# Streams of a recurrence started together, with part of the z terms brought into PSUM by a matrix product

## The chip, the cores and the metric

The program runs on one NeuronCore of a Trainium2 chip. The metric is the device time of one execution in microseconds; the profile is one execution of its own, and its span runs from the first to the last instruction.

## What is computed

The input is x, 32 images of 128 channels by 64 x 64 pixels. A first layer (group norm, a convolution with kernels mixed per image) and a windowed attention layer with layer norms come first. They fill most of the program and are not touched. What the change touches is the last part, cut here from the reference:

```python
Wx = jnp.einsum('bti,hi->bth', x, W)              # 32 images, T = 4096 steps, 128 channels
Wx = ((flat - mean) * rsqrt(var + eps) * gamma + beta).reshape(B, T, H)
def step(yt, wx_t):
    yt = sigmoid(wx_t + yt @ V.T)
    return (yt, yt)
_, ys = lax.scan(step, zeros, swapaxes(Wx, 0, 1))
t = t + ys                                        # added to the result of the layers before
```

Every image is a chain of 4096 steps, one 128 x 128 product and one sigmoid each.

## The kernel before

Before the recurrence the image part writes z (the W product, not yet normalised) to DRAM as z_d and the value to which y is added to the output. The batch norm is folded into a per-channel factor scl and a shift shf.

**by_runs** is the recurrence that runs with these inputs; the other branch, by_steps, is not taken. It cuts the 4096 steps of an image into NRUN = 128 runs of RUN = 32 steps and does all runs at once, each run started WARM = 20 steps early from zero so that it forgets its start. A *group* g is NI = 2 images, so one step handles 128 channels by 2 x 128 values. A group therefore takes 20 + 32 = 52 steps, and there are 16 groups: 832 steps.

A warm step is, after the first one: a TensorE product with fVT (L1914), a VectorE operation that adds scl times z (L1915), and a ScalarE sigmoid (L1916). A kept step is the same on all 256 columns (L1920, L1921, L1924), and a POOL copy (L1925) that puts y over the z it came from. The first warm step is only a sigmoid of z (L1911). y alternates between two tiles, yw[0] and yw[1].

NSTR = 4 *streams* take the groups j, j+4, j+8, j+12 in turn. The order on every queue is the order in which the program emits: a loop calls the streams one after another, one step each. Stream j joins lag = 13 rounds after stream j-1, so the streams stay a quarter of a group apart from beginning to end.

**Transfers.** Six groups have room at a time: five zr tiles and the tile frames. load(g) issues two 2 MB transfers on the SP queue, DRAM to SBUF (L1891). When a group is done, POOL issues two transfers of 2 MB that add the group to the output in DRAM (L1928), and then SP is given load(g + 6), which goes into the tile that these two are still reading. So the chain for every tile is: last copy of group g, its two accumulating transfers, load of group g + 6, first sigmoid of group g + 6 (L1911).

```python
    load(g + NSTR + 2)

live = [stream(j) for j in range(NSTR)]
step = 0
lag = (WARM + RUN) // NSTR
while live:
    for st in list(live[: 1 + step // lag] if step < lag * NSTR else live):
```

Of the kernel before, what the change touches and what calls it, by code (L numbers as in the profile page):

```python
# [8 lines left out]
F32 = mybir.dt.float32  # L9
AF = mybir.ActivationFunctionType  # L10
ALU = mybir.AluOpType
AX = mybir.AxisListType

P = 128
# [19 lines left out]
RUN = 32  # L34
WARM = 20
NRUN = T // RUN
NI = 2
NSTR = 4
# [19 lines left out]
class Clock:  # L58
# [7 lines left out]
    def __init__(self, nc):  # L66
        self.nc = nc
        self.free = {e: 0.0 for e in self.ENGINES.values()}
        self.seen = {}
        self.place = {}  # L70
        self.slots = {}
        self.mode = None
        self.ring = 0.0
        self.port = [[], []]
        self.half, self.edge, self.used = 0, self.WINDOW, 0.0
# [71 lines left out]
    def take(self, eng, pool):  # L147
        t = min(pool, key=lambda t: self.after(eng, t, True))
        pool.remove(t)
        return t  # L150
# [106 lines left out]
def hybrid_kernel(  # L257
# [24 lines left out]
    nc = tc.nc  # L282
# [4 lines left out]
    of = out.rearrange("b c h w -> c b (h w)")  # L287
# [15 lines left out]
    ident = const.tile([P, P], F32, name="ident")  # L303
# [36 lines left out]
    fVT = const.tile([P, P], F32, name="fVT")  # L340
# [12 lines left out]
    with tc.tile_pool(name="sb1", bufs=1) as sb1, tc.tile_pool(  # L353
        name="ps1", bufs=1, space=bass.MemoryType.PSUM
# [32 lines left out]
    with tc.tile_pool(name="sb2", bufs=1) as sb2, tc.tile_pool(  # L387
        name="ps2", bufs=1, space=bass.MemoryType.PSUM
# [1462 lines left out]
    scl = const.tile([P, 1], F32, name="scl")  # L1851
    shf = const.tile([P, 1], F32, name="shf")
# [18 lines left out]
    def by_runs():  # L1871

        with ExitStack() as pb:
            zp = pb.enter_context(tc.tile_pool(name="zp", bufs=NSTR + 1))
            hp = pb.enter_context(tc.tile_pool(name="hp", bufs=1))
            p_v = pb.enter_context(tc.tile_pool(name="p_v", bufs=2, space=bass.MemoryType.PSUM))
            pb.enter_context(tc.manual_schedule())

            NG = NB // NI
            zs = {}

            def load(g):
                if g < NG:
                    if g % (NSTR + 2):
                        zs[g] = zp.tile([P, NI, NRUN, RUN], F32, name="zr")
                    else:
                        zs[g] = framed.rearrange("p i (c r) -> p i c r", r=RUN)
                    for i in range(NI if g else 0):  # L1890
                        nc.sync.dma_start(  # L1891
                            zs[g][:, i].rearrange("p c r -> p (c r)"), z_d[g * NI + i]
                        )

            for g in range(NSTR + 2):
                load(g)

            def stream(j):
                yw = []
                for i in range(2):  # L1900
                    yw.append(hp.tile([P, NI, NRUN], F32, name=f"yw{j}_{i}"))
                    nc.vector.memset(yw[i], 0.0)
                for g in range(j, NG, NSTR):
                    zt = zs[g]
                    if g >= NSTR:
                        for i in range(2):
                            nc.vector.memset(yw[i][:, :, 0:1], 0.0)
                    for r in range(RUN - WARM, RUN):
                        y, z = yw[r % 2][:, :, 1:], zt[:, :, 0 : NRUN - 1, r]
                        if r == RUN - WARM:  # L1910
                            nc.scalar.activation(y, z, AF.Sigmoid, bias=shf, scale=scl)  # L1911
                        else:
                            ps = p_v.tile([P, NI, NRUN], F32, name=f"v{j}")[:, :, 1:]
                            nc.tensor.matmul(ps, fVT, yw[1 - r % 2][:, :, 1:], start=True, stop=True)  # L1914
                            nc.vector.scalar_tensor_tensor(ps, z, scl, ps, ALU.mult, ALU.add)  # L1915
                            nc.scalar.activation(y, ps, AF.Sigmoid, bias=shf)  # L1916
                        yield
                    for r in range(RUN):
                        ps = p_v.tile([P, NI, NRUN], F32, name=f"v{j}")
                        nc.tensor.matmul(ps, fVT, yw[1 - r % 2], start=True, stop=True)  # L1920
                        nc.vector.scalar_tensor_tensor(  # L1921
                            ps, zt[:, :, :, r], scl, ps, ALU.mult, ALU.add
                        )
                        nc.scalar.activation(yw[r % 2], ps, AF.Sigmoid, bias=shf)  # L1924
                        nc.gpsimd.tensor_copy(zt[:, :, :, r], yw[r % 2])  # L1925
                        yield
                    for i in range(NI):
                        nc.gpsimd.dma_start(  # L1928
                            of[:, g * NI + i],
                            zt[:, i].rearrange("p c r -> p (c r)"),  # L1930
                            accum_op=ALU.add,
                            max_dma_last_dim=8192,
                        )
                    load(g + NSTR + 2)

            live = [stream(j) for j in range(NSTR)]
            step = 0
            lag = (WARM + RUN) // NSTR
            while live:
                for st in list(live[: 1 + step // lag] if step < lag * NSTR else live):  # L1940
                    try:
                        next(st)
                    except StopIteration:
                        live.remove(st)
                step += 1

    def by_steps():

# [50 lines left out]
    with tc.If(contr > 0) as arm:  # L1999
        by_runs()  # L2000
# [56 lines left out]
```

## Time and profile before

| what | value |
|---|---|
| device time, three executions | 4645.82, 4645.3, 4629.83 us (median 4645.3) |
| the profiled execution | 4639.78 us |
| its span | 4637.9 us |
| first sigmoid of the recurrence | 4049.6 us after the span's start |
| last sigmoid ends, last accumulating transfer issued | 4611.0 us, 4612.7 us |
| PE, DVE, ACT, POOL busy over the whole span | 90%, 77%, 54%, 36% |

The whole-span shares are averages over the image part (87% of the span) and the recurrence (the last 588 us), so they say nothing on this change. In the recurrence the rows to read are those with lines L1902 to L1928. PE has two records for each product in this data type. "Idle before" counts the time in which the engine had nothing before that row's instructions, with the one that ended it.

### The profile page before, as it was taken

How to read it: one execution, taken by the hardware profiler on the slowest of the kernel's cores; microseconds unless marked ns; L12 is line 12 of the kernel's file. 1: busy time of each engine (PE TensorE's matmuls, PEld its weight loads, DVE VectorE, ACT ScalarE, POOL GpSimd, SP SyncE). 2: the span in 40 equal slices, each digit the busy share in tenths (PEclk: the TensorE clock that was granted, in tenths of full speed). 3: DMA queues.
4: the chain of work that ended last, by engine and by line, in shares of the span. 5: the costliest groups of instructions: out<-in, count | busy, mean ns of one | idle time of the engine just before them, and what ended most of it. 6: DMA issues, size and time to landing. Idle time of an engine off the chain costs nothing.

```text
span 4637.9 us, 102446 instructions
## 1 busy us (share of the span) xinstructions
PE 4195.7 (90%) x41527; PEld 2063.1 (44%) x41527; DVE 3576.6 (77%) x5472; ACT 2503.6 (54%) x4012; POOL 1649.0 (36%) x1656
## 2 busy tenths in 40 slices
PE   3999989999999999999999999999999997389995
PEld 1444444444444444444444444444444443145552
DVE  5877778888878877878887877878788854469994
ACT  0455555555555555545555455555555565258883
POOL 2433333333333333333333333333333321037674
PEclk9999999999999999999999999999999998679997
DMA  3434464554555555555555455555555453439997
GB/s 79 134 120 145 149 198 164 172 175 149 177 167 178 180 161 172 171 163 176 170 177 182 145 190 154 166 173 179 176 159 174 160 182 134 168 151 248 281 263 145
DMA packets 468568, 789.39 MB, mean 170 GB/s; under 512 B 339040, under 2 KB 349296, under 8 KB 435312
## 3 DMA queue, kind: packets, MB, share of 16 engines
q1 hardware_dynamic: 459376, 715.56, 47.3%
q0 software_dynamic: 8704, 67.11, 7.1%
q8 instruction: 332, 5.44, 0.5%
q14 instruction: 156, 1.28, 0.1%
HBM read 499.06 MB, written 276.76 MB: 167 GB/s over the span
## 4 chain that ended last, share of the span: by engine, by line
PE 26%; DVE 15%; DMA 7%; issue 3%; ACT 2%; SPq 2%; POOL 1%; DVEq 0%; ACTq 0%; POOLq 0%
PE nm L241 13%; PE sc L241 6%; PE av L241 4%; DVE v L1921 4%; DVE zt L241 3%; DVE v L1915 2%; SPq L241 2%; DMA place<-r_d 2%; PE v L1920 1%; DMA zr<-z_d 1%; DVE frames L241 1%; DMA place<-x_d 1%; DVE u L241 1%; ACT yw L1924 1%; DMA out_dram<-zr 1%
## 5 line engine op out<-in xcount | busy, mean ns | idle before, releaser
L241 ACT ACTIVATE ex<-sc 128x1152 f32<-128x1152 f32 x896 | 1013.6, 1131 | 879.9 <-PE sc L241 859.3
L241 POOL TENSOR_TENSOR qe<-qs,mqk 128x576 f32<-128x576 f32 x448 | 601.1, 1344 | 864.8 <-PE sc L241 856.3
L241 PE MATMUL nm<-u,w 128*128 128x512 f32 x1536 | 809.1, 631 | 18.9 <-POOL w L241 18.9
L241 PE MATMUL sc<-qe,ks 32*128 32x288 f32 x7168 | 698.0, 459 | 80.4 <-ACT ext L241 33.3
L241 PE MATMUL av<-ex,VE 128*32 128x144 f32 x14336 | 631.0, 294 | 29.7 <-DVE avs L241 29.1
L241 PEld LDWEIGHTS sc<-qe,ks 32*128 32x128 f32 x7168 | 284.9, 185 | 621.5 <-issue 168.0
L241 PEld LDWEIGHTS av<-ex,VE 128*32 128x32 f32 x14336 | 368.1, 110 | 369.1 <-issue 260.8
L241 POOL TENSOR_TENSOR u<-frames 128x528 f32<-128x528 f32 x256 | 374.4, 1475 | 154.8 <-PE nm L241 152.3
L241 PE MATMUL nm<-u,h 128*128 128x512 f32 x768 | 393.0, 620 | 0.0
L241 PEld LDWEIGHTS nm<-u,w 128*128 128x128 f32 x1536 | 253.2, 191 | 276.0 <-issue 245.1
L1920 PE MATMUL v<-yw,fVT 128*128 128x256 f32 x1024 | 327.6, 442 | 40.3 <-ACT yw L1924 39.1
L241 ACT ACTIVATE place<-zt 128x1024 f32<-128x1024 f32 x256 | 264.1, 1054 | 142.4 <-DVE zt L241 121.2
L241 DVE SCALAR_TENSOR_TENSOR u<-u,u 128x528 f32<-128x528 f32 x256 | 263.1, 1044 | 66.8 <-POOL u L241 65.2
L1925 POOL COPY zr<-yw 128x256 f32<-128x256 f32 x416 | 258.7, 689 | 123.4 <-ACT yw L1924 122.7
L1924 ACT ACTIVATE yw<-v,shf 128x256 f32<-128x256 f32 x512 | 242.3, 474 | 106.0 <-DVE v L1921 68.3
L241 PE MATMUL nm<-zt,fWc 128*128 128x512 f32 x512 | 286.5, 651 | 7.8 <-ACT zt L241 6.8
L1921 DVE SCALAR_TENSOR_TENSOR v<-zr,scl,v 128x256 f32<-128x256 f32 x416 | 257.3, 665 | 40.7 <-PE v L1920 40.0
L241 POOL TENSOR_TENSOR kt<-ks,mqk 128x384 f32<-128x384 f32 (+1 forms) x96 | 86.3, 899 | 492.5 <-ACT ks L241 439.4
L241 PE MATMUL nm<-place,avg 128*32 128x256 f32 x3072 | 246.8, 401 | 8.2 <-ACT place L241 7.9
L1914 PE MATMUL v<-yw,fVT 128*128 128x254 f32 x608 | 212.1, 449 | 46.1 <-ACT yw L1911 28.2
L241 DVE SCALAR_TENSOR_TENSOR zt<-sc,gbk,zt 128x576 f32<-128x576 f32 (+1 forms) x192 | 174.9, 911 | 98.0 <-PE sc L241 95.6
L1920 PEld LDWEIGHTS v<-yw,fVT 128*128 128x128 f32 x1024 | 159.8, 194 | 194.6 <-ACT yw L1924 188.3
(205 smaller groups left out, 6676.8 us busy)
## 6 DMA issues: line engine op xcount, KB each, us to landing
place<-r_d SPq DMA_DIRECT2D x384, 512.0 KB
place<-in_conv_k_dram SPq DMA_DIRECT2D x128, 576.0 KB
x_d<-frames SPq DMA_DIRECT2D x32, 2112.0 KB
place<-x_d SPq DMA_DIRECT2D x128, 528.0 KB
frames<-in_x_dram SPq DMA_DIRECT2D x128, 512.0 KB
out_dram<-zt SPq DMA_DIRECT2D x64, 1024.0 KB
z_d<-zt SPq DMA_DIRECT2D x64, 1024.0 KB
zr<-z_d SPq DMA_DIRECT2D x26, 2048.0 KB
```

Of the source, the lines that this page charges most:

```text
L241: got = f(*args, **kw)
L1914: nc.tensor.matmul(ps, fVT, yw[1 - r % 2][:, :, 1:], start=True, stop=True)
L1915: nc.vector.scalar_tensor_tensor(ps, z, scl, ps, ALU.mult, ALU.add)
L1920: nc.tensor.matmul(ps, fVT, yw[1 - r % 2], start=True, stop=True)
L1921: nc.vector.scalar_tensor_tensor(ps, zt[:, :, :, r], scl, ps, ALU.mult, ALU.add)
L1924: nc.scalar.activation(yw[r % 2], ps, AF.Sigmoid, bias=shf)
L1925: nc.gpsimd.tensor_copy(zt[:, :, :, r], yw[r % 2])
```

## The change

The generator function becomes a class Stream, and the order of emission is chosen by an account: four clocks (PE, DVE, ACT, POOL), fixed costs for one operation of each, and a latency. At each turn the operation that can start earliest by this account is emitted, a single engine operation instead of a whole step. Four things differ in what the engines get:

- stream j is entered into the account at 10 us times j, instead of 13 rounds apart;
- a step may have its z term brought in by a second product, of z with dg, a diagonal matrix that holds scl, into the same PSUM tile ahead of the fVT product; the VectorE operation of that step is then left out. Group 0 may do so in any step; the other groups only while such products are at most 0.15 of the steps emitted;
- the two memsets of column 0 between two groups of a stream are emitted right after the last step of the group before, not ahead of the first step of the next;
- dg is made once by VectorE.

Products with fVT, sigmoids, copies, tiles, the pool of five zr tiles, the two accumulating transfers of a group and load(g + NSTR + 2) after them stay as they are.

```diff
+            dg = hp.tile([P, P], F32, name="dg")
+            nc.vector.tensor_scalar_mul(dg, ident, scl)
+            PE, DVE, ACT, POOL, LAT = 0.43, 0.56, 0.46, 0.64, 0.2
+            free = {"PE": 0.0, "DVE": 0.0, "ACT": 0.0, "POOL": 0.0}
...
+                    self.j, self.g, self.k, self.phase = j, j, 0, "ACT"
+                    self.at = 10.0 * j
...
+                def inject(self):
+                    k = self.k if self.phase == "PE" else self.k + 1
+                    c, r, z = self.step(k)
+                    self.ahead = p_v.tile([P, NI, NRUN], F32, name=f"v{self.j}")
+                    nc.tensor.matmul(self.ahead[:, :, c], dg, z, start=True, stop=False)
+                    take("PE", self.read[k % 2] + LAT, PE)
...
+                    if self.phase == "PE":
+                        whole = self.ahead is not None
+                        self.ps = self.ahead if whole else p_v.tile([P, NI, NRUN], F32, name=f"v{self.j}")
+                        self.ahead = None
+                        nc.tensor.matmul(self.ps[:, :, c], fVT, self.yw[1 - r % 2][:, :, c], start=not whole, stop=True)
+                        self.at = take("PE", self.at, PE) + 0.38
+                        self.phase = "ACT" if whole else "DVE"
+                        return
+                    if self.phase == "DVE":
+                        v = self.ps[:, :, c]
+                        nc.vector.scalar_tensor_tensor(v, z, scl, v, ALU.mult, ALU.add)
...
+                    if self.k == WARM + RUN:
+                        g = self.g
+                        for i in range(NI):
+                            nc.gpsimd.dma_start(
...
+                        load(g + NSTR + 2)
+                        self.g, self.k, self.phase = g + NSTR, 0, "ACT"
+                        if self.g < NG:
+                            for i in range(2):
+                                nc.vector.memset(self.yw[i][:, :, 0:1], 0.0)
...
-            live = [stream(j) for j in range(NSTR)]
-            step = 0
-            lag = (WARM + RUN) // NSTR
-            while live:
-                for st in list(live[: 1 + step // lag] if step < lag * NSTR else live):
...
+                    k = st.k if st.phase == "PE" else st.k + 1
+                    if st.ahead is not None or k >= WARM + RUN or (st.g and spent > 0.15 * steps):
+                        continue
+                    at = max(free["PE"], st.read[k % 2] + LAT, st.at if st.k == 0 else 0.0)
+                    if st.phase != "PE" and at + PE > st.due():
+                        continue
+                    if any(o is not st and at + PE > o.due() + 0.2 for o in live):
+                        continue
```

More of the change, by code (lines that the diff above doesn't have):

```diff
@@ L1896, in by_runs @@
                 load(g)
[L1898 to L1911, printed above, removed]
-                        else:
[L1913 to L1934, printed above, removed]
@@ L1936, in by_runs @@
-            live = [stream(j) for j in range(NSTR)]
-            step = 0
-            lag = (WARM + RUN) // NSTR
-            while live:
-                for st in list(live[: 1 + step // lag] if step < lag * NSTR else live):
[L1941 to L1945, printed above, removed]
+            dg = hp.tile([P, P], F32, name="dg")
+            nc.vector.tensor_scalar_mul(dg, ident, scl)
@@ new lines, in by_runs, with take, __init__, step @@
+            PE, DVE, ACT, POOL, LAT = 0.43, 0.56, 0.46, 0.64, 0.2
+            free = {"PE": 0.0, "DVE": 0.0, "ACT": 0.0, "POOL": 0.0}
+            def take(eng, at, cost):
+                at = max(at, free[eng])
+                free[eng] = at + cost
+                return at + cost
+            class Stream:
+                def __init__(self, j):
+                    self.j, self.g, self.k, self.phase = j, j, 0, "ACT"
+                    self.at = 10.0 * j
+                    self.ahead = self.ps = None
+                    self.read, self.kept = [-9.0, -9.0], [-9.0, -9.0]
+                    self.yw = []
+                    for i in range(2):
+                        self.yw.append(hp.tile([P, NI, NRUN], F32, name=f"yw{j}_{i}"))
+                        nc.vector.memset(self.yw[i], 0.0)
+                def step(self, k):
+                    warm = k < WARM
+                    c = slice(1, NRUN) if warm else slice(0, NRUN)
+                    r = RUN - WARM + k if warm else k - WARM
+                    z = zs[self.g][:, :, 0 : NRUN - 1, r] if warm else zs[self.g][:, :, :, r]
+                    return c, r, z
+                def due(self):
+                    if self.phase == "PE":
+                        return self.at
+                    if self.phase == "DVE":
+                        return max(self.at, free["DVE"]) + DVE + ACT + 2 * LAT
+                    return max(self.at, free["ACT"]) + ACT + LAT
+                def inject(self):
[4 more added lines that the diff above has]
+                    take("PE", self.read[k % 2] + LAT, PE)
+                def go(self):
+                    k = self.k
+                    c, r, z = self.step(k)
+                    y = self.yw[r % 2]
+                    if self.phase == "PE":
+                        whole = self.ahead is not None
[5 more added lines that the diff above has]
+                        return
+                    if self.phase == "DVE":
+                        v = self.ps[:, :, c]
+                        nc.vector.scalar_tensor_tensor(v, z, scl, v, ALU.mult, ALU.add)
+                        self.at = take("DVE", self.at, DVE) + 0.25
+                        self.phase = "ACT"
+                        return
+                    if k:
+                        nc.scalar.activation(y[:, :, c], self.ps[:, :, c], AF.Sigmoid, bias=shf)
+                    else:
+                        nc.scalar.activation(y[:, :, c], z, AF.Sigmoid, bias=shf, scale=scl)
+                    end = take("ACT", max(self.at, self.kept[k % 2] + LAT), ACT)
+                    self.read[k % 2] = end
+                    if k >= WARM:
+                        nc.gpsimd.tensor_copy(z, y)
+                        self.kept[k % 2] = take("POOL", end + LAT, POOL)
+                    self.at, self.phase, self.k = end + LAT, "PE", k + 1
+                    if self.k == WARM + RUN:
+                        g = self.g
+                        for i in range(NI):
+                            nc.gpsimd.dma_start(
+                                of[:, g * NI + i],
+                                zs[g][:, i].rearrange("p c r -> p (c r)"),
+                                accum_op=ALU.add,
+                                max_dma_last_dim=8192,
+                            )
+                        load(g + NSTR + 2)
+                        self.g, self.k, self.phase = g + NSTR, 0, "ACT"
+                        if self.g < NG:
+                            for i in range(2):
+                                nc.vector.memset(self.yw[i][:, :, 0:1], 0.0)
+                        else:
+                            live.remove(self)
@@ new lines, in by_runs @@
+            live = [Stream(j) for j in range(min(NSTR, NG))]
+            steps = spent = 0
+            while live:
+                best = None
+                for st in list(live):
+                    at = max(st.at, free[st.phase])
+                    if best is None or (at, st.g) < best[0]:
+                        best = (at, st.g), st, False
+                    k = st.k if st.phase == "PE" else st.k + 1
[6 more added lines that the diff above has]
+                        continue
+                    if (at, st.g) < best[0]:
+                        best = (at, st.g), st, True
+                _, st, ahead = best
+                if ahead:
+                    spent += 1
+                    st.inject()
+                else:
+                    steps += st.phase == "ACT"
+                    st.go()
```

## The prediction

> **What bounds the kernel now.** The change touches nothing before 4046 us, so the whole-span shares are left aside. I read the recurrence in stages (the view of busy time by stretch), then the groups, the chain of waits, and the DMA behind it.
>
> ```profile
> core 0: us, PE busy (x) PEld busy (x) DVE busy (x) ACT busy (x) POOL busy (x), PEclk, DMA share, GB/s
> 4047.90:4082.00 34.10, 15.74 (x26) 6.51 (x26) 8.94 (x16) 7.80 (x15) 0.00 (x0) 0.50 0.99 418
> ...
> 4230.00:4260.00 30.00, 29.48 (x107) 15.80 (x106) 29.81 (x56) 25.39 (x55) 21.70 (x38) 1.00 0.99 252
> ...
> 4615.00:4634.00 19.00, 0.00 (x0) 0.00 (x0) 0.00 (x0) 0.00 (x0) 0.00 (x0) 0.50 1.01 209
> ```
>
> With one stream the engines are half empty and TensorE's clock is 0.50. With four, VectorE is full: some 53 operations in 30 us, one per 0.56 us. But the DMA share is 0.99 in that stretch too. The last row is the accumulating transfer alone, full engines at 209 GB/s: 4.19 MB of a group in 20 us. The loads alone move 418 GB/s: a group in 10 us. Together 30 us of DMA per group, against 52 x 0.56 = 29 us of VectorE. Two limits lie side by side.
>
> ```profile
> L1920 PE MATMUL v<-yw,fVT 128*128 128x256 f32 x1024 | 327.6, 442 | 40.3 <-ACT yw L1924 39.1
> ...
> L1925 POOL COPY zr<-yw 128x256 f32<-128x256 f32 x416 | 258.7, 689 | 123.4 <-ACT yw L1924 122.7
> L1924 ACT ACTIVATE yw<-v,shf 128x256 f32<-128x256 f32 x512 | 242.3, 474 | 106.0 <-DVE v L1921 68.3
> ...
> L1921 DVE SCALAR_TENSOR_TENSOR v<-zr,scl,v 128x256 f32<-128x256 f32 x416 | 257.3, 665 | 40.7 <-PE v L1920 40.0
> ```
>
> These are the prices of a step. The chain shows where the other limit already ends last:
>
> ```profile
> 4404.76 1.75 POOL zr L1925 x3
> 4406.51 0.59 POOL out_dram L1928
> 4407.10 34.95 DMA out_dram<-zr
> ...
> 4442.54 24.64 DMA zr<-z_d
> ...
> 4467.29 0.82 ACT yw L1911
> ```
>
> This is one tile changing hands: out in 35 us, reload in 25 us, then the first sigmoid. It waited only 0.64 us, because the streams are a quarter of a group apart and there is time for this.
>
> [...] a load beside an accumulate takes 24.6 us here, and 10 us of transfer alone. [...] all 32 transfers share that one queue; here they do follow each other. [...] Here a stop of 2.39 us at 4317.07 was followed by 0.50 from 4317.5 to 4324. [...] z is read at steps of 128 bytes, and L1911, which reads it, takes 815 ns where L1916 from PSUM takes 473. No run here shows TensorE reading it so.
>
> **The change, part by part.** I number the 832 sigmoids of the changed program in ScalarE's order.
>
> *Ramp.* Before, three joins of 13 rounds; sigmoid 212 starts at 4214.1. In the new order streams 1, 2, 3 join at sigmoids 8, 20, 35, and group 0 has 51 injected z products. One stream alone costs 2.52 us a step (1.22 PE + 0.65 DVE + 0.47 ACT + gaps); injected, 1.22 + 0.47 + 0.08 = 1.77. So 7 steps cost 12 us; the next 12 and 15, with two and three streams, about 10 and 9. For the 177 steps to sigmoid 211: VectorE 144 x 0.56 = 81 us; TensorE 176 + 31 = 207 products at 0.43 = 89 (in the chain two products back to back took 1.71 us at half clock, 0.86 each; half of that at full clock), POOL 113 x 0.56 = 63. None is met exactly by an order made from fixed costs; I take 0.57 a step, 101. Sum 132 us, so sigmoid 211 ends near 4182 instead of 4214: **32 us gained**. The loads of groups 1 to 3 land about 10 us apart from 4058 on, before their streams ask.
>
> *Injection later.* 74 products in the other groups take 74 of 765 VectorE operations away. It is worth something only where VectorE is what is short. Of the steps that count below, 171 have 157 VectorE operations (93 us at 0.54 a step), 172 have 144 (90 us; TensorE 195 x 0.43 = 84), 146 have 123, with only three streams for the last 53 (81 us). Sum **264 us**, against 489 x 0.56 = 274 at the old pace. The injected product costs 0.43 us if the step of 128 bytes is free, and up to 0.86 if not: 74 x 0.43 = 32 us more at worst, partly in TensorE's idle time; I take none.
>
> *Streams close together.* In the new order group 0 ends at sigmoid 144, group 1 at 211, group 2 at 228, group 3 at 247. Stream 3 then starts group 7 at sigmoid 248. But group 7 lies in group 1's tile, and SP may load it only when group 1's accumulate is done. From sigmoid 211: the last pair took 24.8 us from the end of its sigmoid (4610.97) to landing, 0.4 for SP, and then a load that shares the engines with group 2's accumulate, 24.6: **50 us**. The 37 steps between need 21 us. So ScalarE stops at L1911 for some 29 us, and all four streams stop with it: behind it in ScalarE's queue are their sigmoids, for which TensorE, VectorE and POOL wait. It repeats for group 11 (group 5 ends at 419, wanted at 455) and group 15 (627, 666): three holds of 50 us that cover 37, 36 and 39 steps. Groups 6, 10, 14 are wanted 85 to 92 steps after their tile's end, some 47 us, and need 25 + 13: they pass. [...]
>
> *End.* Before, one group's accumulate stands after the last sigmoid: 27 us to the end of the span. In the new order group 13 ends at sigmoid 812, 14 and 15 within 20 more: three pairs of 21 us in one queue, with 2.7 us ahead and 2.5 behind, so the end is 812 plus **70 us**.
>
> *Small ones.* dg: one VectorE operation beside the loads; twelve pairs of memsets that now wait in VectorE's queue for the last POOL copy, about 1.3 us each: nine fall within or beside a hold, the others in the rounding; up to 4 us. POOL's two transfer issues (1.4 us) are 32 as before. SP issues the same 30 loads.
>
> *Sum.* 4049.6 + 132 + 150 + 264 + 7.5 + 70 = 4673 us of span, 35 over 4637.9. The profiled execution was 5.5 us below the median, so against the median 4645.3 the forecast is **4680 us**, 0.75% slower.
>
> **Rivals.** (a) *The reload is in time: faster.* If tile 1 came back within the 37 steps, each hold would shrink from 50 to 21 us: 4673 - 3 x 29 - 7.5 = 4578 of span, 4586. For it: the account spreads the ends of streams 0 and 1 over 67 steps. Against it: the chain's 35 + 25 us. It decides if out and reload take under 21 us; even without a neighbour they need 24.8 + 13. Chance 0.07. (b) *Holds, but all terms favourable: the same.* Ramp 126, holds 47, 489 steps with VectorE exactly full (424 operations x 0.56 = 237) plus 6, end 68: 4049.6 + 126 + 141 + 237 + 6 + 68 = 4628 at the extreme; about half-way, 4650, is within reach. For it: VectorE is 99% busy now in a fixed order. Chance 0.25 for within 0.5%, which is 23 us and about what a measurement of this kernel can tell from no change. (c) *TensorE becomes the bound*: strided z at 0.86 makes group 0's ramp 51 x 0.43 = 22 us longer and the rest up to 32: 4680 + 40 = 4720. It speaks for it that L1911 is slow on the same read, against it that nothing shows TensorE so. It is within the slower case. (d) The change may not do what it says: the order shows 125 products with dg, so that is excluded; that 51 are in group 0, with VectorE far from full there, limits what they can bring.
>
> **Numbers.** My forecast, holds and a longer end beating the shorter ramp: 0.68. The same: 0.25; faster: 0.07. The range: ramp 126 to 142, holds 141 to 153, steps 250 to 285, restarts 3 to 12, end 68 to 74 give 4637 to 4716 if all agree; with the offset to the median and a chance for (c), 4640 to 4714.
>
> **What would show it.** Sigmoid 212 near 4182. L1911 with a wait of 25 to 35 us for DMA, three times, at group 7, 11, 15, where now the longest is 2.4; a clock of 0.50 after each. VectorE under 90% in the rest. After the last sigmoid 45 to 60 us of transfers alone where there were 25. I am wrong if L1911's waits for DMA sum to under 40 us, or if the steps between the holds cost over 0.6 us, which would be TensorE.

## The result, and the profile after

The changed kernel takes **4724.1 us** (median of 4, 4714.9 to 4727.9) against 4645.6 for the kernel before (4629.8 to 4648.7): the ratio is 1.0168, with a 95% interval of 1.0146 to 1.0189. It is slower, as forecast, but by 79 us where the forecast said 35, and above the range of 4640 to 4714. Its profiled execution has a span of 4713.1 us.

The first sigmoid stands at 4045.5 us in this profile and at 4049.6 in that of before; the image part ahead of it is the same in both, and its time moves by some us from run to run. So I count from the first sigmoid to the end of the span: **588.4 us before, 667.6 after**. The 832 sigmoids, counted along ScalarE's order in the trace, cut this into the stages of the prediction (its 271.5 us are 264 for the steps and 7.5 for three restarts at a low clock, 2.5 us each, an estimate of mine that no trace had shown).

| stage (sigmoids) | before | after | predicted |
|---|---|---|---|
| ramp (1 to 212) | 164.5 | 145.6 | 132 |
| three holds (212 to 249, 420 to 456, 628 to 667) | 63.3 | 152.9 | 150 |
| between them (249 to 420, 456 to 628, 667 to 813) | 295.4 | 303.3 | 271.5 |
| from sigmoid 813 to the end | 65.1 | 65.8 | 70 |

The holds alone are 90 us longer. The ramp gives 19 us back, not 32; the stretches between, where injection was to save VectorE's time, cost 8 us more than before. The same view of busy time by stretch as shown of before, now of the kernel after:

```profile
core 0: us, PE busy (x) PEld busy (x) DVE busy (x) ACT busy (x) POOL busy (x), PEclk, DMA share, GB/s
4049.00:4182.00 133.00, 132.74 (x481) 88.64 (x480) 83.55 (x143) 89.67 (x193) 61.69 (x103) 0.99 0.54 191
...
4302.00:4342.00 40.00, 39.77 (x149) 26.69 (x148) 31.77 (x57) 30.51 (x67) 30.38 (x52) 1.00 0.79 211
...
4674.00:4712.00 38.00, 0.00 (x0) 0.00 (x0) 0.00 (x0) 0.00 (x0) 2.48 (x3) 0.50 0.97 200
```

Before, VectorE was full (29.81 of 30 us). In the second row, a stretch with injection, it has fallen to 31.77 of 40 us, 79%. TensorE's busy share says little here: it is 99% and more in both rows, but it was 29.48 of 30 us before as well, because the records overlap (one lasts 0.38 us and more, and the next starts 0.216 us after its start in the median). Counting starts says more. Where nothing holds it up, a product with fVT is followed after 0.43 us, and one with dg after 0.84 (shown below). Before, 107 records are 53.5 products in 30 us, so TensorE needed 77% of the time. In the second row there are 10 products with dg and 64.5 with fVT, which need 36 of 40 us, 90%. Work did go from one engine to the other, but the other became the shorter one. The last row is the end: 38 us of accumulating transfers with only POOL's last issues beside them.

Three of the costliest groups of the page:

```profile
L1952 PE MATMUL v<-yw,fVT 128*128 128x256 f32 (+1 forms) x1632 | 438.9, 406 | 103.0 <-ACT yw L1965 88.3
L1958 DVE SCALAR_TENSOR_TENSOR v<-zr,scl,v 128x256 f32<-128x256 f32 (+1 forms) x605 | 364.8, 667 | 208.4 <-PE v L1952 206.0
L1963 ACT ACTIVATE yw<-v,shf 128x256 f32<-128x256 f32 (+1 forms) x816 | 374.3, 472 | 154.7 <-DVE v L1958 84.4
```

Read the last column. The idle time of TensorE, 103 us, was ended for 88.3 us by L1965, a group's first sigmoid. VectorE, which had next to no idle time before while four streams ran (8.7 of the 379 us from 4141 to 4520), waited 206 us for products, 88 of them in the three holds. And who ended L1965's own wait is in the view of that line; below it is the same line of the kernel before, L1911:

```profile
L1965 ACT ACTIVATE yw<-zr,shf,scl x13: 807/815/854, 4055.8 to 4551.9; 128x254 f32<-128x254 f32 x13
...
its engine sat idle before it (us, times) until:
  DMA zr<-z_d: 87.2, 3
```

```profile
L1911 ACT ACTIVATE yw<-zr,shf,scl x13: 811/814/842, 4082.6 to 4496.9; 128x254 f32<-128x254 f32 x13
...
its engine sat idle before it (us, times) until:
  DMA zr<-z_d: 4.0, 3
```

Three waits, 87.2 us together where there were 4.0. The chain of waits around the first of them shows the tile that changes hands:

```profile
4191.13 0.62 POOL zr L1969
4191.75 0.29 issue
4192.04 0.73 POOL out_dram L1975
4192.77 22.49 DMA out_dram<-zr
...
4215.78 26.25 DMA zr<-z_d
...
4242.14 0.82 ACT yw L1965
```

Group 1 ends, the second of its two accumulating transfers lands 22.5 us after its issue, the reload of the tile takes 26.3 us, and then group 7's first sigmoid can run: 51 us from sigmoid 212. Before, the chain in the prediction was even longer, 35 + 25 us, but there the sigmoid at its end was wanted only some 60 us after the tile's last copy. Here it was wanted after 37 sigmoids, which take 21 us where nothing stops them.

What injection costs is seen in the order of time on TensorE, in us, with duration and number of records:

```profile
4310.73 0.70 PE L1952 MATMUL v<-yw,fVT 128*128 128x256 f32 x2
4311.27 1.02 PE L1940 MATMUL v<-zr,dg 128*128 128x254 f32 x2
4312.11 0.82 PE L1952 MATMUL v<-yw,fVT 128*128 128x254 f32 x3
```

From the start of the product with dg (L1940) to the start of the one behind it are 0.84 us. Of the 125 products with dg, 120 ran at full clock, and the median of this distance is 0.85 us. A product with fVT is two records too, and one record follows the other after 0.216 us in the median, so 0.43 us a product.

### The profile page after: what moved, and what is told of

Same layout as the page of the kernel before. It is cut to its first block, busy times and chain, and to the rows that moved or that the text cites. A ratio compares the mean times of both kernels' runs of the same rounds, so it can differ in the third digit from the quotient of the medians.

```text
span 4713.1 us, 102792 instructions
## 1 busy us (share of the span) xinstructions
PE 4223.0 (90%) x41777; PEld 2148.1 (46%) x41777; DVE 3514.9 (75%) x5348; ACT 2490.0 (53%) x4012; POOL 1641.4 (35%) x1656
## 4 chain that ended last, share of the span: by engine, by line
PE 63%; DVE 14%; DMA 11%; issue 3%; ACT 3%; SPq 2%; POOL 2%; DVEq 0%; ACTq 0%; POOLq 0%
PE nm L241 32%; PE sc L241 13%; PE av L241 10%; PE v L1952 6%; DVE zt L241 5%; DMA place<-r_d 3%; SPq L241 2%; PE v L1940 2%; DVE frames L241 2%; DMA zr<-z_d 2%; DMA out_dram<-zr 1%; ACT ex L241 1%; DVE u L241 1%; DVE v L1958 1%; DMA place<-x_d 1%
## 5 line engine op out<-in xcount | busy, mean ns | idle before, releaser
L1952 PE MATMUL v<-yw,fVT 128*128 128x256 f32 (+1 forms) x1632 | 438.9, 406 | 103.0 <-ACT yw L1965 88.3
L1958 DVE SCALAR_TENSOR_TENSOR v<-zr,scl,v 128x256 f32<-128x256 f32 (+1 forms) x605 | 364.8, 667 | 208.4 <-PE v L1952 206.0
L1963 ACT ACTIVATE yw<-v,shf 128x256 f32<-128x256 f32 (+1 forms) x816 | 374.3, 472 | 154.7 <-DVE v L1958 84.4
L1952 PEld LDWEIGHTS v<-yw,fVT 128*128 128x128 f32 x1632 | 290.9, 195 | 280.6 <-ACT yw L1963 124.7
L241 ACT COPY zt<-nm 128x512 f32<-128x512 f32 x256 | 149.5, 585 | 176.8 <-PE nm L241 175.8
```

Source lines behind the costliest of these rows:

```text
L241: got = f(*args, **kw)
L1952: nc.tensor.matmul(self.ps[:, :, c], fVT, self.yw[1 - r % 2][:, :, c], start=not whole, stop=True)
L1958: nc.vector.scalar_tensor_tensor(v, z, scl, v, ALU.mult, ALU.add)
L1963: nc.scalar.activation(y[:, :, c], self.ps[:, :, c], AF.Sigmoid, bias=shf)
```

## The experiments

There are two suspects: the holds, and the price of the product with dg. The rivals are that the order made by the account costs by itself, and that the transfers' total throughput stops the streams. Times are medians against the kernel before on the same chip; stage times are from one profiled execution each, counted as above. The ramp, which is the same program in the changed kernel, in no_out_1_5_9 and in group0_only, took 145.6 us in each of the three, so a stage that waits for no transfer repeats far better than whole executions, which spread over 10 us and more; a hold differs by about 1 us between the kernels that have it.

**no_out_1_5_9**: takes away what the three loads wait for. The kernel leaves three groups out of its output.

```diff
-                        for i in range(NI):
+                        for i in range(0 if g in (1, 5, 9) else NI):
                             nc.gpsimd.dma_start(
```

> Edit: the accumulating transfers of groups 1, 5 and 9 are left out (their y is not added to the output), so that the loads of groups 7, 11 and 15 need not wait for them; 6 of 32 transfers are gone, everything else stays. Theory (a hold is accumulate, then reload, of one tile): these loads go out right at the end of the group before, land some 14 us later, and are wanted after 21 us: L1965 waits under 5 us in place of 87 in all, the clock stays at 1.00, the span falls by about 85 us to 4628 (4618 to 4640). Rival (the stops come from the transfers' total throughput): three of sixteen groups' accumulates are 63 us of transfer, the waits fall by about a third, span 4670 to 4690.

Measured: 4629.5 us, ratio 0.9966 (0.9957 to 0.9974); 575.2 us from the first sigmoid, 92.4 less than the changed kernel. The three holds fell from 152.9 to 65.4 us, ramp and end stayed (145.6, 65.6), the stretches between fell by 5 us. The view of L1965 names no transfer any more:

```profile
its engine sat idle before it (us, times) until:
  DVE yw L1918: 1.8, 1
```

The throughput rival predicted a third of the waits gone; all are. A hold is one tile's accumulate and reload. The 5 us in the stretches between are what three restarts at a low clock cost: this kernel's clock stays at 1.00 from 7 us after the first sigmoid to 10 us before the last one ends, where the changed kernel's was still 0.50 for 5 to 6 us after each hold.

**z_contiguous**: the price of the product, with the same tile read without the step.

```diff
+                    w = NRUN - c.start
+                    flat = zs[self.g].rearrange("p i c r -> p i (c r)")
+                    z = flat[:, :, r * NRUN : r * NRUN + w]
                     nc.tensor.matmul(self.ahead[:, :, c], dg, z, start=True, stop=False)
```

> Edit: the product with dg reads as many columns, but a contiguous run of the z tile in place of one value in 32 (so the z terms of these 125 steps are other values); order, counts and transfers stay. Theory (the strided read doubles the price of the product with dg): its two records start 0.41 and 0.43 us apart now; they fall to 0.21 each, 0.42 us less a product. 51 of them lie in the ramp and 59 outside the three holds, so 46 us come back: span 4667 us (4658 to 4678) where the changed kernel has 4713. Rival (the fixed order, not the price of the product, slows the steps): records fall, the span stays within 8 us of 4713.

Measured: 4734.7 us, ratio 1.0196 (1.0179 to 1.0213). That is neither theory's number. The waits of this kernel show what I had overlooked:

```profile
PEld v L1943 <- POOL zr L1972: 46.4, 34, 5.3
...
PE v L1943 <- POOL zr L1972: 33.1, 30, 4.9
...
PEld v L1943 <- POOL frames L1972: 30.2, 38, 4.4
...
PE v L1943 <- POOL frames L1972: 14.5, 24, 4.0
```

A contiguous run of the z tile crosses the columns of many steps, and POOL writes y into those. So TensorE waited for copies that have nothing to do with the step (us in total, times, longest). The time of the whole is therefore inconclusive. The records are not: where no wait came between, the second record of a product started 0.214 us after the first and the next product 0.214 us after that, on the very tile zr where the changed kernel has 0.41 and 0.43.

**z_still**: the same question with data that nobody writes.

```diff
+            still = frames[:, 1, T : T + NI * NRUN].rearrange("p (i c) -> p i c", i=NI)
...
-                    nc.tensor.matmul(self.ahead[:, :, c], dg, z, start=True, stop=False)
+                    nc.tensor.matmul(self.ahead[:, :, c], dg, still[:, :, c], start=True, stop=False)
```

> Edit: the product with dg reads 256 contiguous values per partition that nobody writes in this part (the end of the tile frames, past its 4096 columns), in place of z at one value in 32; the 125 steps so lose their z term; order, counts and transfers stay, and no wait is added as it was in z_contiguous. Times from the first sigmoid on, where the changed kernel has 667.6 us. Theory (the strided read doubles the price): the product falls from 0.85 to 0.43 us; the ramp to sigmoid 212 falls from 145.6 to about 130, the three stretches between the holds from 303 to about 282, holds stay at 51 each; 630 us (620 to 640). Rival (the order, not the price): 660 to 668.

Measured: 4683.2 us, ratio 1.0084 (1.0068 to 1.0101); 630.3 us from the first sigmoid, where the theory said 630. The ramp took 130.4, the holds 152.5, the stretches between 281.5. In TensorE's order of time:

```profile
4303.25 0.59 PE L1941 MATMUL v<-frames,dg 128*128 128x254 f32 x2
4303.68 3.60 PE L1953 MATMUL v<-yw,fVT 128*128 128x254 f32 x14
```

4303.68 less 4303.25 is 0.43 us. So with the read at steps of 128 bytes the product takes twice as long, 0.84 us against 0.43, and that alone is 37 of the 667.6 us. That it is the step and not the tile read is seen in z_contiguous, where the z tile itself gave the short distance.

**group0_only**: is injection outside group 0 worth anything?

```diff
-                    if st.ahead is not None or k >= WARM + RUN or (st.g and spent > 0.15 * steps):
+                    if st.ahead is not None or k >= WARM + RUN or st.g:
```

> Edit: only group 0 may inject; 51 products with dg instead of 125. Start of the streams, holds and ends stay at almost the same sigmoids. Theory (an injected product costs TensorE 0.85 us and saves VectorE 0.56 us, and TensorE is the shorter one): the 490 steps outside ramp and holds run at 0.56 us plus 7.5 us of cold clock, 282 us instead of 303; span about 4690 us (4683 to 4698), three holds of 51 us as they were. Rival (taking work from VectorE is worth its 0.56 us): 59 more VectorE operations cost up to 33 us, span 4713 to 4745.

Measured: 4709.6 us, ratio 1.0138 (1.0121 to 1.0155); 655.4 us from the first sigmoid, 12 less than the changed kernel. The second hold now sits one sigmoid later, inside the next stretch, so I take holds and stretches together: 440.2 us against 456.2, 16 less, where the theory said 21 (cut at the shifted places, the holds are 153.0 and the stretches 287.2); the end is 4 us longer, since groups 13 and 14 end six sigmoids and one later in this order. The direction is the theory's: the 74 products of the later groups cost time, they save none. The intervals of the two ratios overlap (1.0155 is the upper end here, 1.0146 the lower end of the changed kernel), so this rests on the stage times. From sigmoid 212 to the end the changed kernel takes 522.0 us, this one 509.9, and z_still, with the same 74 products at the short price, 499.8. So later injection loses 12 us at the price it has and would gain 10 at the other.

**apart24**: no injection, streams 24 us apart in the account.

```diff
-                    self.at = 10.0 * j
+                    self.at = 24.0 * j
...
-                    if st.ahead is not None or k >= WARM + RUN or (st.g and spent > 0.15 * steps):
+                    if True:
```

> Edit: the account's order without injected products, and the streams 24 us apart in it instead of 10. A tile's next group is now wanted 88 steps, 49 us, after its group before has ended. Theory (spacing decides over the holds): out and reload take 38 us alone and 50 with a neighbour, so L1965 waits for DMA 0 to 10 us in all; pace 0.56 us a step; the ramp is a little shorter than the one of the kernel before, which has 33 us between its streams; span 4615 to 4640 us, equal to or a little under 4638. Rival (an order from an account costs by itself against one step per stream in turn): over 4660.

Measured: 4645.8 us, ratio 1.0004 (0.9994 to 1.0014); 593.5 us from the first sigmoid, at the edge of the theory's range (a span of 4640.2 us). L1965 still waited 5.5, 8.1 and 8.2 us, twice what I allowed, so 88 steps are not quite enough. But with every transfer in place the waits fell from 87.2 to 21.8 us; leaving out the later injection alone, in group0_only, had left them at 89.3. The rival is answered too: with the streams apart and no injection, an order made by the account is as fast as one step per stream in turn.

**both_b**: both suspects away, in a kernel that leaves out three groups of the output and 125 z terms.

> Edit: z_still and no_out_1_5_9 together (the 125 injected steps lose their z term, the outputs of groups 1, 5 and 9 are not added). Theory (holds and the price of the product with dg are all that the changed kernel loses, and they lie one after the other): from the first sigmoid 667.6 us, less 92.4 for the holds, less 37.3 for the product, 538 us (530 to 546); ratio to before 0.988 to 0.991. Rival (a third limit close behind, as VectorE full or transfers): 555 to 575.

Measured: 4589.9 us, ratio 0.9881 (0.9865 to 0.9898); 535.3 us from the first sigmoid, the theory's 538 within 3. The two losses add up, and no third limit of the size that the rival named stands behind them.

**ramp1, ramp2, ramp2_lag12**: keep what helped. The kernel before with its own order, and z injected only where few streams are at work. The core of ramp2:

```diff
+            def value(ps, y, z):
+                few = now["n"] <= 2 and now["at"] == 0
+                if few:
+                    nc.tensor.matmul(ps, dg, z, start=True, stop=False)
+                nc.tensor.matmul(ps, fVT, y, start=not few, stop=True)
+                if not few:
+                    nc.vector.scalar_tensor_tensor(ps, z, scl, ps, ALU.mult, ALU.add)
...
-                for st in list(live[: 1 + step // lag] if step < lag * NSTR else live):
+                turn = list(live[: 1 + step // lag] if step < lag * NSTR else live)
+                for at, st in enumerate(turn):
+                    now["n"], now["at"] = len(turn), at
```

ramp1 has `now["n"] == 1` there; ramp2_lag12 is ramp2 with `lag = 12`.

> Edit: the kernel before, in its own order of rounds and 13 rounds between the streams; a step brings its z in with a product with dg, in place of the VectorE operation, only while one stream alone is at work (13 rounds at the start, 13 at the end). Theory (an injected product is worth its cost only where TensorE and VectorE idle, and no hold arises while the streams stay a quarter of a group apart): 24 steps at 1.5 us (7 took 10.3 us in the changed kernel) in place of 2.5; 24 us less, less 3 us of transfer at the end, where the last two groups come closer; from the first sigmoid 588 falls to about 567, the ratio to before 0.9955. Rival (the transfers are the bound from the first output on, so an earlier start turns into waits of L1911): 580 to 588.

> Edit: as ramp1, and with two streams at work the first of the two injects as well. Theory: besides, TensorE stays busy enough to keep its clock at 1.00 through the ramp, so that a round of two streams costs 1.95 us in place of 2.47 at the start (13 rounds, 7 us), and some 5 us at the end; from the first sigmoid about 556 us, ratio 0.993. L1911 waits under 12 us in all. Rival (transfers become the bound): no better than ramp1, more waits of L1911.

> Edit: as ramp2 with 12 rounds between the streams instead of 13. Theory: one round of few streams less at three places at each end, some 6 us; but a tile's next group is wanted 24 rounds, 54 us, after its group before has ended, and out and reload take 50 to 60 with neighbours: waits of L1911 grow to 10 to 20 us in all. About equal to ramp2, 552 to 566 us from the first sigmoid. Rival (spacing does not matter until 50 us): 550.

Measured: ramp1 4617.4 us, ratio 0.9941 (0.9929 to 0.9953), 560.3 from the first sigmoid (567 expected); ramp2 **4605.3 us, ratio 0.9922 (0.9909 to 0.9935)**, 554.3 (556 expected); ramp2_lag12 4612.4 us, ratio 0.9932 (0.9919 to 0.9945), without a profile, so that its waits are not known. ramp2 beats both kernels of this study, by 40 us and by 119. Its two ends and a stretch of its middle, in the view of busy time by stretch:

```profile
4045.00:4085.00 40.00, 39.71 (x118) 22.59 (x119) 7.11 (x11) 16.78 (x35) 3.21 (x5) 0.94 1.00 426
4130.00:4260.00 130.00, 127.47 (x457) 68.11 (x455) 129.06 (x239) 110.58 (x233) 93.25 (x155) 1.00 0.85 218
4540.00:4570.00 30.00, 27.88 (x84) 14.17 (x82) 4.55 (x7) 11.91 (x26) 17.73 (x27) 1.00 0.83 168
```

Beside them, the end of the kernel before with one stream left:

```profile
4580.00:4612.00 32.00, 14.04 (x25) 5.66 (x24) 8.41 (x13) 6.16 (x13) 10.42 (x16) 0.56 0.66 132
```

In the first 40 us the granted clock is 0.94, where the kernel before had 0.50; in the middle nothing has changed, VectorE is full; at the end the clock holds at 1.00 where it was 0.56. L1923, a group's first sigmoid here, waits for transfers only 3.7 us in all. The intervals of ramp2 and ramp2_lag12 overlap: whether 12 rounds are a loss against 13 is not settled. Those of ramp1 and ramp2 overlap a little as well, but the ramp to sigmoid 212 took 152.9 us in ramp1 and 145.1 in ramp2, 8 us less where 7 were expected.

## Why the prediction was wrong in size and right in direction

Against the prediction the ramp came out 13.6 us longer, the holds 2.9, the stretches between 31.8, and the end 4.2 us shorter. These 44 us are the difference between the 35 us of the forecast and the 79 measured. (Its two sums against the median, 4680 and 4586, are one or two us above what they add up to, which changes nothing.)

**Right: the holds.** Three of them, at groups 7, 11 and 15, 51.0, 50.9 and 51.0 us long where the prediction had 50 each, and right in their parts: in the first one it was 24.2 us from the end of sigmoid 211 to the landing and 26.3 for the reload, where the prediction had 24.8 and 24.6. Groups 6, 10 and 14 passed without a wait, as written. no_out_1_5_9 shows the cause.

**Right in the main: the clock and the end.** The granted clock went to 0.50 in each hold and back to 1.00 some 5 to 6 us after the start of the sigmoid that ended it (4242.1 to 4247.2, 4394.8 to 4400.8 and 4551.9 to 4557.8). A restart cost less than the prediction's estimate of 2.5 us, though: without holds the stretches between are 4.7 us shorter (no_out_1_5_9 against the changed kernel) and 4.8 us (both_b against z_still), 1.6 us a restart. From sigmoid 813 to the end it was 65.8 us against 70. But that this is a loss was my error of view: before, the same stage takes 65.1, since there the streams run out one by one while the outputs drain. The longer drain is paid for by a shorter run-down. Transfers alone after the last sigmoid took 39.8 us, not the 45 to 60 that the prediction had as a sign.

**Wrong: the term for the injected product.** The prediction wrote "The injected product costs 0.43 us if the step of 128 bytes is free, and up to 0.86 if not" and "I take none". Its 0.86 was an estimate, twice the 0.43, that no trace of TensorE had shown. Measured it is 0.84. This is the step that failed. The term was mis-sized in two places, since the ramp's sum has all its products at 0.43 too, and z_still measures both: 15 us of the ramp (145.6 against 130.4; predicted 132) and 22 us of the stretches between (303.3 against 281.5; predicted 271.5). Together 37 of the 45 us by which these two stages were underestimated. With the short price the prediction's gain from later injection, 274 less 264 us, would have come: from sigmoid 212 on, z_still is 10 us ahead of group0_only. The prediction also had a sign for this, steps between the holds at over 0.6 us, "which would be TensorE", and they took 0.62 (303.3 us for 489). The rival that held it, TensorE as the bound, had given 4720 us, close to what came; of its 22 and up to 32 us it had counted 40, and 37 were measured. I had put it inside the slower case instead of giving it the chance that the slow strided read of L1911 argued for.

**Wrong: the pace without it.** The rest is in the steps: even with the product at 0.43 us, the stretches between took 281.5 us against 271.5; without holds and so without restarts (both_b) they took 276.8 against the 264 of the steps alone. The prediction had taken 0.52 to 0.56 us a step on the ground that VectorE had fewer operations; in both_b they came out at 0.57 on average. It is not injection that keeps them there: in group0_only, with none, the stretches took 287.2 us for 490 steps, 0.58 a step after three restarts are taken off. A stretch of z_still with injection shows how close two engines are to full:

```profile
4390.00:4440.00 50.00, 49.73 (x212) 36.29 (x211) 45.45 (x80) 41.75 (x93) 30.08 (x53) 1.00 0.72 213
```

Counted by starts, 212 records at 0.215 us are 46 of 50 us of TensorE, and 80 operations at 0.56 us are 45 of VectorE. What takes the rest no run here shows; that the order was fixed by other durations than the real ones is only a guess.

**The one favourable rival**, that reloads come in time, was rightly excluded by the chain; had they come in time, as in no_out_1_5_9, the changed kernel would have been 0.3% faster, not the 1.3% that I gave this rival; most of what is missing is the price of the product, since both_b, without that too, is 1.2% faster.

## What to carry to other kernels

Before moving an operation from a full engine to an idle one, price it with its own access pattern: here TensorE had room for a product of 0.43 us (10 us gained), not for one of 0.84 (12 us lost). Where buffers go through out and reload, count the work between the end of a buffer's old content and the first use of its new one; streams that are moved closer together shorten that, and in a queue that is served in order the one that is late stops all of them (here for 27.7 to 29.9 us, three times). A way of working that does not pay in a full stretch may pay at its ends, where the engines have time to spare: the same product, put only there, made this kernel 0.8% faster than before.

## What the runs showed of the hardware that was not expected

The product with dg, its moving operand read at steps of 128 bytes, took 0.84 us for 254 columns where contiguous columns took 0.43 (z_still), a factor of two at full clock. At half clock the factor is gone: 0.86 to 0.87 us in the four such products of the changed kernel that followed one another closely, against 0.85 in the four of z_still and, in the median, for contiguous products with fVT in the kernel before (4318.5 to 4323.6 us, clock 0.50). ScalarE took 815 ns for a sigmoid of z at that step and 473 from PSUM; there the memory differs as well as the step, so the step's share is not shown.

The clock of TensorE rose 7 us after the first sigmoid when a single stream also injected (4052.7 in the changed kernel), and stayed at 0.50 for 60 us in the kernel before, where one and two streams left TensorE only partly filled (15.74 of 34.10 us busy with one, 23.70 of 27.00 with two). In ramp1, where only the single stream injects, it rose 6 us after the first sigmoid, fell to 0.50 at 4078.4 us, just as the second stream joined (4078.8), and was back at 4112.5, just after the third had (4111.7). ramp2, whose clock stayed up with two streams, is 6 us shorter than ramp1; that the clock alone made this was not tried apart.

The clock fell after short stops too: TensorE stood still for 1.77 and 2.15 us in ramp2 (to 4292.34 and to 4412.18) and for 2.51 us in the kernel before (to 4317.94), and the clock was then 0.50 for 3.4, 3.4 and 6.8 us. Three stops of 1.7 us in z_contiguous left it at 1.00.
